# A recurrence's gradient is centred as its last step instead of its first, and an output operand is built by one operation and four copies

## The chip, the cores and the metric

The kernel runs on one core of a Trainium2 chip. Its engines work side by side, each through its own queue in order: TensorE (PE) multiplies matrices, VectorE (DVE), ScalarE (ACT) and GpSimd (POOL) work on elements, SyncE (SP) and some of the others start DMA transfers. The metric is the time of one execution on the device in microseconds, median of several runs. Before the change it is 1993.64 us, the median of 3 runs that lie between 1992.97 and 1996.19 us.

## The reference

Two layers, each `x + attention(norm(x)) + ffn(norm(x))`, all in fp32. The change touches only the first layer's attention, a recurrence ("test-time training") over 32 blocks of 16 tokens, for 4 sequences and 32 heads of width 16:

```python
def step(carry, x):
    W1_s, b1_s = carry
    xq, xk, xv, eta_mb = x
    Z1 = xk @ W1_s + b1_s
    grad = _ln_fused_l2_bwd(Z1, xv - xk, ln_w, ln_b)
    Attn1 = jnp.tril(xq @ xk.swapaxes(-1, -2))
    b1_bar = b1_s - jnp.tril(eta_mb) @ grad
    Z1_bar = xq @ W1_s - eta_mb * Attn1 @ grad + b1_bar
    last_eta = eta_mb[:, :, -1, :, None]
    W1_new = W1_s - (last_eta * xk).swapaxes(-1, -2) @ grad
    b1_new = b1_s - jnp.sum(last_eta * grad, axis=-2, keepdims=True)
    out = xq + _ln(Z1_bar, ln_w, ln_b)
    return ((W1_new, b1_new), out)
```

with the gradient of a layer norm and a squared error:

```python
def _ln_fused_l2_bwd(x, target, gamma, beta):
    mu = x.mean(-1, keepdims=True)
    std = jnp.sqrt(x.var(-1, keepdims=True) + EPS)
    xh = (x - mu) / std
    gxh = (gamma * xh + beta - target) * gamma
    return (D * gxh - gxh.sum(-1, keepdims=True) - xh * (gxh * xh).sum(-1, keepdims=True)) / (D * std)
```

The rest of the first half of the kernel is a gated FFN (hidden size 1408) and the projections around the recurrence. The second layer is an attention with 16 heads over 1024 tokens per pass and a mixture of experts; the change does not touch it.

## The kernel before

**Two stages.** Until about 970 us the kernel computes layer 1; from there, layer 2. Layer 1 goes through the tokens in 8 chunks of 64 tokens of each of the 4 sequences. Every chunk gives 4 steps of the recurrence, 32 steps (n = 0 to 31) in all. The state is small, so a step has few matrix multiplications and a long chain of element operations. The chunk's other work (FFN, projections, post norm of the chunk before) is cut into pieces by generators (`gate_up`, `down`, `keys`, `token_tile`, `queries`, `finish`) and put between the step's parts: `fill(us)` takes pieces from the list until their nominal PE times reach `us`.

```python
for n in range(NM):
    wh = weights_out(n)
    pz = first_product(n, pre)
    po = queries_out(n, wh)
    g = gradient(n, pz, pre)
    gh = out_operands(n, g, pz)
    fill(gaps[0])          # 11 us of other PE work
    update(n, g, pre)
    fill(gaps[1])          # 3 us
    emit_out(n, po, gh)
    fill(gaps[2])          # 8 us
    pre = prepare(n + 1)   # once its chunk's operands are there
```

**One step.** `weights_out` copies the state out of PSUM (tile `wacc`, L332 and L335). `first_product` gives `pz`, the values z beside the attention products, in one PSUM tile (matmuls `pz<-gsum` and `pz<-wq_bd,sk`). `queries_out` starts the output in PSUM tile `pso`. `gradient` (L353 to L391) makes the gradient from z on DVE, with two calls of ACT (a square, L360, and a square root, L364). Each group of 16 values is centred first (L356, L358), then scaled, multiplied by gamma squared and added to the target part (`kv`, L379); then two sums (L382) are taken out (L386 to L388). `update` copies the gradient into the block-diagonal operand `g_bd` (L395, two copies on DVE, two on ACT) and multiplies it into the state (`wacc<-g_bd,km`). `out_operands` makes the two operands of the step's output: `gh` (L421, two POOL operations, one for each half of the head pair, gradient times mask `m2`), and `a_bd` (L424, four DVE operations of 32 partitions each, that add 1 to the attention products in `pz`, multiply them by the negative causal mask `mneg` and put them on a block diagonal). `emit_out` multiplies them (`pso<-a_bd,gh`) and DVE takes the result out (`zch` L449, `bias_o` L450).

**Around it.** `prepare` (L303 to L326) makes the next step's operands on POOL: the DMA `kv<-rows` (L307, on POOL's queue, three buffers), `sk` (L314), the copies of the queries into `wq_bd` (L316, they wait until `queries_out` of the step before has read the old ones) and `km` (L321). At the end of a chunk POOL starts the DMAs `z<-zch` (L454) and `zb<-z` (L456), which bring the recurrence's outputs into another layout. `finish` of that chunk then runs in the next one: ACT squares `zb` (`pn_sq`, L549), PE sums the squares (`pj<-pn_sq,bones`), ACT takes the root (L554), and so on. `gate_up` multiplies into PSUM tile `pf` (two buffers); ACT (`sg`, L477) and DVE (`hid`, L478) empty it.

**What sets the order.** The program above is not the order of the queues. A scheduler reorders each engine's instructions when the kernel is built, by its own estimates of their durations and waits; only those given to `keep_in_program_order` are fixed. So a change in one function can move the instructions of others, on all queues.

## Time and profile before

| what | value |
|---|---|
| median of 3 runs | 1993.64 us |
| the profiled execution's own time | 1996.04 us |
| its span, first to last instruction | 1994.3 us |
| PE busy | 1938.3 us (97%), 11626 matmuls |
| DVE busy | 1169.6 us (59%) |
| ACT busy | 816.1 us (41%) |
| POOL busy | 528.2 us (26%) |
| PE busy, 0 to 100 us | 91.1 us |
| PE busy, 100 to 900 us | 770.1 us |
| PE busy, 900 to 1000 us | 90.6 us |
| PE busy, 1000 us to the end | 986.4 us of 994 |

The span is what the profiler saw of one execution, from the first instruction to the last; the execution's own time lies 1.7 us above it. A busy share is an average; what an engine waits for is read from the waits (engine, line and tile that waited, what released it, total, number, longest) and from the timeline (start, duration, instruction, and in brackets the idle time ahead of it with what ended it). The trace has two matmul records for each fp32 matmul of the program.

### The profile page before, as it was taken

The numbers are of one execution on the slowest core, as the hardware profiler recorded it, in microseconds if no ns is written. First come the engines' busy times: TensorE is split into PE (matmuls) and PEld (weight loads), VectorE is DVE, ScalarE is ACT, GpSimd is POOL, SyncE is SP. The second block draws the span as 40 slices with busy tenths as digits, with TensorE's granted clock in tenths as the row PEclk, the third lists the DMA queues.
The fourth block names the chain that finished last, engine by engine and source line by source line (L and its number), as shares of the span: only waits on it lengthen the run. The fifth ranks groups of instructions, "written<-read, shape, count | busy, mean of one in ns | idle before, by whom it ended". The sixth has DMA issues, their size and how long they took to land.

```text
span 1994.3 us, 32414 instructions
## 1 busy us (share of the span) xinstructions
PE 1938.3 (97%) x11626; PEld 1233.3 (62%) x11626; DVE 1169.6 (59%) x2579; ACT 816.1 (41%) x1695; POOL 528.2 (26%) x643
## 2 busy tenths in 40 slices
PE   8999999999999999998999999999999999999999
PEld 6777676767766676753777744555555555555555
DVE  4445748466666657474555656556555655655565
ACT  2234333334433443422222155455545545555552
POOL 5333343424333342512000101111211121222223
PEclk9999999999999999999999999999999999999999
DMA  6757566646456455745651135444344444333344
GB/s 170 210 130 209 143 185 167 175 120 179 141 145 189 126 173 159 224 128 195 225 168 49 58 94 141 118 106 104 101 111 108 103 110 108 95 101 98 89 115 117
DMA packets 226924, 273.51 MB, mean 137 GB/s; under 512 B 88587, under 2 KB 117452, under 8 KB 226124
## 3 DMA queue, kind: packets, MB, share of 16 engines
q1 hardware_dynamic: 204928, 237.19, 43.3%
q0 software_dynamic: 9760, 28.41, 5.0%
q10 hardware_dynamic: 12076, 5.84, 1.0%
q8 instruction: 93, 1.52, 0.3%
q14 instruction: 67, 0.55, 0.1%
HBM read 174.18 MB, written 34.87 MB: 105 GB/s over the span
## 4 chain that ended last, share of the span: by engine, by line
PE 49%; DVE 1%; DMA 0%; ACT 0%; issue 0%; SPq 0%; DVEq 0%; ACTq 0%
PE pc L1254 11%; PE sc L1207 9%; PE pq L1184 8%; PE px L1301 5%; PE p L1301 4%; PE pk L1184 3%; PE epg L976 3%; PE epo L1039 1%; PE epu L976 1%; PE eox L1069 1%; PE pvo L891 1%; PE pw L866 1%; PE eo L1069 1%; DMA gu<-in_gu 0%; DVE st L1225 0%; ACT prob L1227 0%
## 5 line engine op out<-in xcount | busy, mean ns | idle before, releaser
L1225 DVE TENSOR_REDUCE st<-sc 128x1 f32<-128x512 f32 x256 | 168.9, 681 | 244.0 <-PE sc L1207 244.0
L1227 ACT ACTIVATE prob<-sc,st 128x512 f32<-128x512 f32 x256 | 175.1, 686 | 210.5 <-DVE st L1225 210.3
L1254 PE MATMUL pc<-prT,lv 128*128 128x512 f32 x512 | 230.8, 593 | 0.0
L1232 ACT ACTIVATE prob<-prob,st 128x512 f32<-128x512 f32 x256 | 181.9, 720 | 58.8 <-DVE st L1231 58.8
L1236 DVE STREAM_TRANSPOSE tt<-prob 128x512 f32<-128x512 f32 x256 | 178.4, 700 | 43.0 <-ACT prob L1232 36.5
L117 PE MATMUL pf<-xT,wg 128*128 128x256 f32 x704 | 175.6, 391 | 6.2 <-DMA wg<-in_wg 4.4
L1184 PE MATMUL pq<-cq,uq 128*128 128x512 f32 x384 | 175.2, 592 | 0.0
L117 PE MATMUL pf<-xT,wu 128*128 128x256 f32 x704 | 167.6, 381 | 1.5 <-DMA wu<-in_wu 1.5
L117 PE MATMUL pd<-wd,hid 128*128 128x512 f32 x352 | 166.1, 600 | 1.3 <-DMA wd<-in_wd 1.2
L1254 PEld LDWEIGHTS pc<-prT,lv 128*128 128x128 f32 x512 | 96.4, 190 | 100.1 <-issue 98.1
L117 PEld LDWEIGHTS pf<-xT,wg 128*128 128x128 f32 x704 | 133.2, 194 | 33.5 <-issue 4.7
L1207 PE MATMUL sc<-k,q 32*128 32x512 f32 x1024 | 145.7, 617 | 2.5 <-ACT prob L1227 2.5
L117 PEld LDWEIGHTS pf<-xT,wu 128*128 128x128 f32 x704 | 134.5, 191 | 20.5 <-DMA wu<-in_wu 1.9
L478 DVE SCALAR_TENSOR_TENSOR hid<-pf,us,sg 128x256 f32<-128x256 f32 x88 | 42.0, 478 | 156.9 <-ACT sg L477 156.4
L1184 PEld LDWEIGHTS pq<-cq,uq 128*128 128x128 f32 x384 | 74.1, 193 | 90.7 <-issue 90.0
L314 POOL TENSOR_SCALAR sk<-k,m 128x256 f32<-128x256 f32 x64 | 61.2, 968 | 179.9 <-PE pz L117 167.7
L1195 POOL TENSOR_TENSOR kr<-kr,t2k 128x512 f32<-128x512 f32 x16 | 20.3, 1270 | 332.3 <-DVE t2k L1194 332.3
L421 POOL TENSOR_SCALAR gh<-grad,m 128x256 f32<-128x256 f32 x64 | 61.2, 966 | 154.5 <-DVE grad L390 131.6
L117 PEld LDWEIGHTS pd<-wd,hid 128*128 128x128 f32 x352 | 63.4, 190 | 60.2 <-issue 43.8
L1207 PEld LDWEIGHTS sc<-k,q 32*128 32x128 f32 x1024 | 48.4, 185 | 82.7 <-issue 73.2
L477 ACT ACTIVATE sg<-pf,gs 128x256 f32<-128x256 f32 x88 | 41.6, 473 | 132.8 <-PE pf L117 132.3
L1256 ACT COPY ctxT<-pc 128x512 f32<-128x512 f32 x64 | 37.4, 585 | 127.2 <-PE pc L1254 127.1
(316 smaller groups left out, 3467.9 us busy)
## 6 DMA issues: line engine op xcount, KB each, us to landing
prT<-tt SPq DMA_DIRECT2D x992, 64.0 KB, 2.0
wd<-in_wd SPq DMA_DIRECT2D x176, 256.0 KB, 3.1
wg<-in_wg SPq DMA_DIRECT2D x88, 256.0 KB, 3.0
wu<-in_wu SPq DMA_DIRECT2D x88, 256.0 KB, 3.1
cq<-lat_d SPq DMA_DIRECT2D x48, 256.0 KB, 3.8
rows<-rows SPq DMA_DIRECT2D x128, 66.0 KB, 2.2
kv<-rows POOLq DMA_DIRECT2D x32, 264.0 KB, 4.1
gu<-in_gu SPq DMA_DIRECT2D x3, 2048.0 KB
```

The costliest lines, as they stand in the source:

```text
L117: nc.tensor.matmul(out, lhsT=lhsT, rhs=rhs, start=start, stop=stop, skip_group_check=True)
L314: nc.gpsimd.tensor_scalar_mul(sk[:, :, :, h, :], at(k1[ch], slice(0, P)), m2[:, h : h + 1])
L421: nc.gpsimd.tensor_scalar_mul(gh[:, :, h, :], g, m2[:, h : h + 1])
L976: nc.tensor.matmul(ps, lhsT=w[:, c, :], rhs=x[:, c], start=start and c == 0, stop=c == 1, skip_group_check=True)
L1184: nc.tensor.matmul(ps, lhsT=columns(ws[hg][w]), rhs=x, start=(i == 0), stop=(i == len(srcs) - 1))
L1207: nc.tensor.matmul(ps[h], lhsT=qk[f"q{c}"][r, i * P : (i + 1) * P], rhs=qk[f"k{c}"][r, :], start=(n == 0), stop=(n == 2),)
L1225: pin(nc.vector.tensor_reduce(mx, ps[h], AX.X, ALU.max, negate=True))
L1227: pin(nc.scalar.activation(pr, ps[h], AF.Exp, bias=mx, scale=1.0, accum_out=sm))
L1232: pin(nc.scalar.mul(pr, pr, sm))
L1236: nc.vector.transpose(out=tt[:, :, h - 2], in_=pr.rearrange("p (k kq j) -> p kq k j", kq=4, j=32))
L1254: pin(nc.tensor.matmul(pc, lhsT=lv[:, b, k, :], rhs=at[:, :, k, :], start=(k == 0), stop=(k == E - 1)))
L1301: nc.tensor.matmul(ps[:, q, :], lhsT=a[:, k, q * P : (q + 1) * P], rhs=w[:, k, :], start=start and k == 0 and q == 0, stop=k == 1, skip_gr ...
```

## The change

The gradient is computed in another order. Before, z is centred, squared and scaled, and the mean of the gradient is taken out ahead of the part along z. After, z is squared as it comes out of PSUM; the part along z is taken out first; and the mean of what remains is taken out as the last step. The state W and the bias start centred (`centre(w0)`, `centre(b0)`, L729 to L737, there before the change too), and a gradient that is centred in its last step keeps them so up to rounding, so that z has mean zero without being centred. The two sums, one reduction of 128 x 512 elements before, become two of 128 x 256.

`a_bd` is made by one DVE operation over all 128 partitions into a new tile `at`, and four copies of 32 partitions, two on ACT and two on POOL. `gh` is made by one POOL operation over 512 elements instead of two over 256.

```diff
         def gradient(n, pz, pre):
             z = pz[:, :, :HD]
-            s = wk.tile([P, NG], F32, tag="s", name=f"s_{n}")
-            nc.vector.tensor_reduce(s, z, AX.X, ALU.add)
             xh = wk.tile([P, NG, HD], F32, tag="xh", name=f"xh_{n}", bufs=1)
-            nc.vector.scalar_tensor_tensor(xh, spread(s), -1.0 / HD, z, ALU.mult, ALU.add)
             sq = wk.tile([P, NG, HD], F32, tag="sq", name=f"sq_{n}", bufs=1)
-            nc.scalar.activation(sq, xh, AF.Square)
+            nc.scalar.activation(sq, z, AF.Square)
...
-            nc.vector.tensor_mul(xh, xh, spread(r))
+            nc.vector.tensor_mul(xh, z, spread(r))
...
-            nc.vector.tensor_reduce(
-                s12.rearrange("p k g -> p (k g)"), pair.rearrange("p k g d -> p (k g) d"), AX.X, ALU.add
-            )
+            nc.vector.tensor_reduce(s12[:, 1], pair[:, 1], AX.X, ALU.add)
+            nc.vector.tensor_mul(xh, xh, spread(s12[:, 1]))
             u = wk.tile([P, NG, HD], F32, tag="u", name=f"u_{n}", bufs=1)
-            nc.vector.scalar_tensor_tensor(u, spread(s12[:, 0, :]), -1.0 / HD, pair[:, 0], ALU.mult, ALU.add)
-            nc.vector.tensor_mul(xh, xh, spread(s12[:, 1, :]))
-            nc.vector.scalar_tensor_tensor(u, xh, -1.0 / HD, u, ALU.mult, ALU.add)
+            nc.vector.scalar_tensor_tensor(u, xh, -1.0 / HD, pair[:, 0], ALU.mult, ALU.add)
+            nc.vector.tensor_reduce(s12[:, 0], u, AX.X, ALU.add)
+            nc.vector.scalar_tensor_tensor(u, spread(s12[:, 0]), -1.0 / HD, u, ALU.mult, ALU.add)
...
         def out_operands(n, g, pz):
             gh = wk.tile([P, NG, 2, HD], F32, tag="gh", name=f"gh_{n}")
-            for h in range(2):
-                nc.gpsimd.tensor_scalar_mul(gh[:, :, h, :], g, m2[:, h : h + 1])
-
+            nc.gpsimd.tensor_mul(
+                gh,
+                g.unsqueeze(2).to_broadcast([P, NG, 2, HD]),
+                m2.unsqueeze(1).unsqueeze(3).to_broadcast([P, NG, 2, HD]),
+            )
+            at = wk.tile([P, NG, K], F32, tag="at", name=f"at_{n}", bufs=1)
+            nc.vector.scalar_tensor_tensor(
+                at, pz[:, :, HD:], 1.0, mneg.unsqueeze(1).to_broadcast([P, NG, K]), ALU.add, ALU.mult
+            )
             for be, r in enumerate(quarters):
-                nc.vector.scalar_tensor_tensor(
-                    a_bd[r, :, be, :K],
-                    pz[r, :, HD:],
-                    1.0,
-                    mneg[r].unsqueeze(1).to_broadcast([32, NG, K]),
-                    ALU.add,
-                    ALU.mult,
-                )
+                (nc.scalar.copy if be < 2 else nc.gpsimd.tensor_copy)(a_bd[r, :, be, :K], at[r])
             return gh
```

## The prediction

> **What bounds the kernel now.** I read the page's first part, then TensorE's waits, then the timeline around the long ones.

> ```profile
> PE 1938.3 (97%) x11626; PEld 1233.3 (62%) x11626; DVE 1169.6 (59%) x2579; ACT 816.1 (41%) x1695; POOL 528.2 (26%) x643
> ```

> TensorE is the bound. Only its idle time can be won or added to; the second stage (from 970 us) idles some 10 us in all, and the changed kernel's instruction order, read beside the old one, differs nowhere in it. What TensorE waits for in most of the recurrence (190 to 960 us; total, times, longest):

> ```profile
> PE pj L117 <- ACT pn_sq L549: 5.9, 2, 3.1
> PE pso L117 <- POOL gh L421: 5.8, 4, 2.7
> PE wacc L117 <- DVE g_bd L395: 3.7, 3, 1.7
> PE wacc L117 <- ACT g_bd L395: 1.9, 3, 1.0
> PE pz L117 <- ACT wq_bd L332: 1.8, 2, 1.1
> PE pf L117 <- DVE hid L478: 1.5, 2, 1.1
> ```

> The chain that the change shortens ends in `gh` and `g_bd`: 11.4 us of waits over ten steps. In the other steps filler covers it. Here step 7, TensorE's timeline:

> ```profile
> 264.15 0.48 PE L117 MATMUL pso<-a_bd,gh 128*32 128x68 f32 x17 [2.72 <-POOL gh L421]
> ...
> 267.34 1.93 PE L117 MATMUL pz<-wq_bd,sk 128*32 128x128 f32 x32 [0.79 <-ACT wq_bd L332]
> ...
> 270.05 2.90 PE L117 MATMUL pf<-xT,wg 128*128 128x256 f32 x8
> 274.52 1.89 PE L117 MATMUL pf<-xT,wg 128*128 128x256 f32 x8
> ```

> After the wait of 2.72 the matmuls run slow: 2.90 us for eight against 1.89 later, and `pz` takes 1.93 against 1.08 in other steps. From 265.3 to 272.8 that is 3.0 us lost to the clock on top of the wait. Waits of 2.39 (at 51 us) and 2.23 (at 159) were followed by 2.6 and 1.8 lost; those of 2.2 (at 600) and 3.06 (at 819) by none.

> **The change part by part.** Durations are the groups' means.

> *Gradient.* Gone: sum and centring of z (0.42 each), the double sum (0.68). New: two sums of the shape of L362 (0.42 each), and `at` (0.42), which the new order puts into the chain behind the scaling of `xh`; the four `a_bd` operations were in DVE's pauses. So 1.52 leaves and 1.25 enters: the gradient comes 0.3 us earlier. Where no table load stands between square and root (14 of 32), two `a_bd` operations had also held up the reciprocal (step 31: 0.55 us), so there 0.8. DVE loses 4 x 0.42 + 1.52 - 1.25 = 1.95 us a step, 62 us in all, worth nothing by itself, since TensorE covers it.

> *`gh`.* Two operations of 0.97 become one over 512 elements. POOL's tensor-tensor rows of that size take 1.27 to 1.29 (L495, L496, L1195), two operations with the mask 1.93. I take 1.29, the same operation and count: `gh` comes 0.64 earlier than the gradient gives; at 1.93, not at all.

> *Copies.* Two more on ACT (0.40, row L395) and two on POOL (0.43, row L316). Their readers come later than `gh` in nearly all steps, and the order puts POOL's ahead of `gh`, in its idle time: nothing. They wait for `at`; behind ACT's wait stand table loads and `sg`, which come about 0.2 later, with TensorE a `pf` buffer ahead: nothing. The worst case is 2 us each at the two waits for `hid`.

> *Buffers.* `pz` is held until `at`, 1 us longer, but the next `pz` is 15 us off: nothing.

> *What the chain wins.* Steps 6, 14, 18, 23 lose their waits for `g_bd` (0.5, 1.0, 1.0, 0.5). Step 7: `gh` is 1.0 earlier and the new order has two more matmuls (0.87) ahead of it: 1.85 of 2.72, and the 3.0 of slow clock. `gh` in 13, 17, 21: 0.4, 0.4, 0.9 (fillers ahead of it shrink by 0.3 to 2.3). Step 10: 0.5, since 1.74 of filler leaves. The wait for `hid` in step 12: 0.9, as `hid` now stands ahead of the last gradient operation. Step 30, for a norm: 0.4. Sum: 3.0 + 4.85 + 1.7 + 0.5 + 0.9 + 0.4 = **11.35 won**.

> *What the order loses.* The scheduler moved three things on other queues.

> Step 24: one `pj<-pn_sq` matmul now stands right behind `pso<-wq_bd`, ahead of the gate matmuls.

> ```profile
> 707.29 0.63 PE L117 MATMUL pso<-wq_bd,wh 128*32 128x64 f32 x32
> 716.74 0.65 PE L117 MATMUL wacc<-g_bd,km 128*32 128x64 f32 x32 [1.72 <-DVE g_bd L395]
> 717.82 1.99 PE L117 MATMUL pf<-xT,wg 128*128 128x256 f32 x8 [0.43 <-DVE hid L478]
> ```
> ```profile
> 710.80 1.06 ACT L549 ACTIVATE pn_sq<-zb 128x1024 f32<-128x1024 f32 x1 [0.25 <-DMA zb<-z]
> ```

> `pn_sq` waits for a DMA that the change does not speed up and ends at 711.9; TensorE is there at 707.9: a wait of 4.0, with every later matmul behind it, for 1.72 + 0.43 that go. Net 1.85, and the slow clock.

> Step 28: POOL's `kv` DMA for this very step moves behind two more copies and two `sk` operations.

> ```profile
> 814.27 0.84 POOL L316 COPY wq_bd<-q 32x256 f32<-32x256 f32 x2 [3.87 <-PE pso L117]
> 815.06 0.55 POOL L307 DMA_DIRECT2D kv<-rows  x1
> 816.61 1.82 POOL L314 TENSOR_SCALAR sk<-k,m 128x256 f32<-128x256 f32 x2
> ```
> ```profile
> 818.17 0.18 DVE L367 TENSOR_TENSOR rl<-r,kv 128x16 f32<-128x16 f32 x1 [0.69 <-DMA kv<-rows]
> ```
> ```profile
> 819.53 1.12 PE L117 MATMUL pj<-pn_sq,bones 128*128 128x512 f32 x2 [3.06 <-ACT pn_sq L549]
> 827.49 0.65 PE L117 MATMUL wacc<-g_bd,km 128*32 128x64 f32 x32
> 827.96 0.66 PE L117 MATMUL pso<-a_bd,gh 128*32 128x68 f32 x32
> ```

> Four copies from 814.27 end at 815.95, two `sk` at 817.85; `kv` then lands 3.1 later (815.06 to 818.17 before), at 820.95, and DVE, waiting at L367, holds all behind it. The gradient takes 4.4 more: 825.3. On POOL `km` twice two (2.0, 2.1) and two DMAs (0.6 each) follow `kv`'s landing, then `gh`: 827.5. TensorE reaches the first `pso<-a_bd,gh`, which the new order puts ahead of 16 gate matmuls (6.9 us), at about 818.6, and stands 8.9 us. These, `wacc` and the other outputs then end at 835.5 instead of 828.55; one `pn_sq` matmul (0.87) is done earlier and one of 0.43 later, which leaves **5.7 lost** (with `gh` at 1.93: 6.3).

> Step 25: 0.76 less filler against a gradient that is not earlier, as DVE does the post norm between: 0.6.

> The clock after waits of 4.0 and 8.9: between 0 (the rows of 2.2 and 3.06) and 3.0 each; 3.0 is the row after the longest wait that slowed, and I take it twice. Lost: 1.85 + 5.7 + 0.6 + 6.0 = **14.15**.

> **The sum.** 14.15 - 11.35 = 2.8 us slower: 1998.8 for the profiled execution's 1996.04, which lies 2.4 over the median. On the median: 1996.4. Unseen small losses in an order rewritten on five queues are likelier than unseen gains (all gains lie in the listed waits), so I say **1997.0**.

> [...]

> **Rivals.** *The chain wins.* If the waits at 24 and 28 cost no clock (0 twice) and `kv` in step 28 is no later than before, the losses are 1.85 + 0.6 and about 2 for the moved output matmul: 11.35 - 4.45 = 7 faster, 1986.7. For it: the 3.06 row had no slow clock. Against it: POOL's queue is in order, and `kv` stands behind 2.7 us of named work. It decides at a `kv` landing before 819.

> *`gh` is dear and the clock stays slow.* At 1.93 the gains of 7, 13, 21 shrink by 0.64 each and step 28 loses 0.6 more; with one more slow-clock stretch (3.0) from a new wait, 2.8 + 2.5 + 3.0 = 8.3 slower, 2002. For it: a mask operand, as L421 has; against: the rows of equal operation.

> *The steps all stay covered*, gains and losses both half: 1.4 slower, 1995.

> **How the numbers follow.** 0.2% is 4 us, about what a measurement of this kernel can tell from no change: 1989.65 to 1997.63. The sum with its spread (1993 to 2001) has 0.45, split 0.23 within, 0.22 slower; the chain wins 0.25 (0.02 of it within); the dear `gh` 0.22, slower; all covered 0.08, 0.07 of it within. Faster 0.23, same 0.32, slower 0.45 (0.22 + 0.22 + 0.01). The range leaves out 0.1 on each side: 1987, the chain's win in full, and 2004, the dear case and 2 more.

> **What would show it.** Right: in TensorE's waits a new `pj <- ACT pn_sq` of about 4 us in step 24 and a `pso <- POOL gh` of 8 to 9 in step 28, slow matmuls behind both; `g_bd` waits below 2 us in sum; `gh` at 1.3; the time at DVE down by 62 us with no gain of its own. Wrong: `gh` waits gone altogether, or a chain from `pz` to the gradient that is not shorter (7.8 us in step 12), or new waits for `hid`.

## The result and the profile after

The changed kernel takes 2018.51 us in the median (2015.08 to 2019.25, 4 runs) against 1994.69 for the kernel before (1992.97 to 1996.19, 4 runs): a ratio of 1.0116, 95% interval 1.0099 to 1.0134. It is 23.8 us slower where the prediction's sum had 2.8. Its profiled execution has a span of 2016.6 us, 22.3 more than the one of before. The first part of its page:

```profile
PE 1937.2 (96%) x11626; PEld 1233.8 (61%) x11626; DVE 1132.6 (56%) x2451; ACT 839.2 (42%) x1757; POOL 532.5 (26%) x675
```

TensorE's busy time is the same to 1.1 us (1938.3 before). The whole loss is idle time of TensorE. DVE has 37 us less to do (62 were expected), and that bought nothing, as expected. TensorE's waits from 190 to 960 us (total, times, longest), the view shown for before:

```profile
PE pj L117 <- ACT pn_sq L544: 14.4, 4, 4.5
PE pso L117 <- POOL gh L416: 11.3, 3, 8.9
PE pf L117 <- DMA wg<-in_wg: 4.9, 2, 2.5
PE wacc L117 <- DVE g_bd L391: 3.8, 5, 1.8
PE pf L117 <- DVE hid L473: 2.3, 1, 2.3
```

`pn_sq` went from 5.9 to 14.4, `gh` from 5.8 to 11.3, `hid` from 1.5 to 2.3 (and a wait of 5.5 at 66 us, ahead of this window). `g_bd`, which the change was to shorten, went from 5.6 (3.7 and 1.9) to 3.8. So the chain's waits did shrink, and waits that are not the chain's grew.

Four steps lose 24.3 us between them, what precedes the first step loses 3.9, and the other steps win some of it back. The length of a step here is the time from the end of its `pz` matmuls to the end of the next step's, read off the timelines. The number behind x on TensorE's lines counts records, two for each of these matmuls.

**Step 28** is 12.3 us longer. TensorE, POOL and DVE, from their timelines:

```profile
829.55 1.98 PE L117 MATMUL pj<-pn_sq,bones 128*128 128x512 f32 x4 [2.49 <-ACT pn_sq L544]
840.48 0.43 PE L117 MATMUL pso<-a_bd,gh 128*32 128x68 f32 x2 [8.95 <-POOL gh L416]
840.85 3.78 PE L117 MATMUL pf<-xT,wg 128*128 128x256 f32 x8
844.42 2.13 PE L117 MATMUL pf<-xT,wu 128*128 128x256 f32 x8
```
```profile
826.29 1.93 POOL L314 TENSOR_SCALAR sk<-k,m 128x256 f32<-128x256 f32 x2
828.17 1.15 POOL L307 DMA_DIRECT2D kv<-rows  x2
```
```profile
834.09 0.17 DVE L364 TENSOR_TENSOR rl<-r,kv 128x16 f32<-128x16 f32 x1 [6.66 <-DMA kv<-rows]
```

This is the predicted place: `kv` behind four copies and two `sk`, DVE standing on it for 6.66 us, and one output matmul (of 16) ahead of the gate matmuls, which holds all of them for 8.95 us (8.9 were predicted). The gate matmuls behind it run at half clock (3.78 us for eight records against 1.89; the granted clock is 0.50 until 844.9).

**Step 4** is 5.2 us longer, and the prediction had nothing there. POOL, ACT and TensorE:

```profile
183.13 0.98 POOL L426 COPY a_bd<-at 32x256 f32<-32x256 f32 x2 [8.17 <-DVE at L422]
184.17 1.98 POOL L316 COPY wq_bd<-q 32x256 f32<-32x256 f32 x4
186.25 2.07 POOL L314 TENSOR_SCALAR sk<-k,m 128x256 f32<-128x256 f32 x2
188.26 0.62 POOL L307 DMA_DIRECT2D kv<-rows  x1
188.88 0.78 POOL L451 DMA_DIRECT2D zb<-z  x1
```
```profile
194.74 1.06 ACT L544 ACTIVATE pn_sq<-zb 128x1024 f32<-128x1024 f32 x1 [6.04 <-DMA zb<-z]
```
```profile
195.84 3.31 PE L117 MATMUL pj<-pn_sq,bones 128*128 128x512 f32 x4 [4.54 <-ACT pn_sq L544]
```

POOL stands 8.17 us on `at` with the two new copies at the head of its queue. Behind them wait four copies, two `sk`, `kv` and the transfer of `zb`, which needs none of them. In the kernel before, `zb` was issued at 179.51, 5.9 us after the step's `pz`; here it is 9.1 us after. POOL and TensorE before:

```profile
179.51 0.78 POOL L456 DMA_DIRECT2D zb<-z  x1
```
```profile
185.78 1.98 PE L117 MATMUL pj<-pn_sq,bones 128*128 128x512 f32 x4 [0.93 <-ACT pn_sq L549]
```

**Step 0** is 3.9 us longer: TensorE waits 5.53 us for `hid`, and the next eight records take 3.68. DVE's order puts that `hid` behind the gradient, and the gradient waits 3.67 us for `kv`. TensorE and DVE:

```profile
66.62 3.68 PE L117 MATMUL pf<-xT,wg 128*128 128x256 f32 x8 [5.53 <-DVE hid L473]
```
```profile
59.25 0.18 DVE L364 TENSOR_TENSOR rl<-r,kv 128x16 f32<-128x16 f32 x1 [3.67 <-DMA kv<-rows]
```

**Step 8** is 2.9 us longer by a wait for `hid` too (2.34), there without a wait for `kv`.

A further 3.9 us are lost **ahead of step 0**, where no instruction's place differs. DVE's norm statistics wait for a transfer of the input until 19.75 us (they start at 17.98 before). An operation on `lrb` then takes 4.08 us beside three memsets of POOL (0.15 before, where it ended ahead of them; its line stands in the last section). TensorE waits 1.89 and 0.83 us for `rows`, which stand behind it on DVE, and its granted clock is 0.50 from 29.1 to 32.5 us. That the change makes the transfer late is not shown.

### The profile page after: what moved, and what is told of

Same layout as the page of the kernel before. It is cut to its first block, busy times and chain, and to the rows that moved or that the text cites. A ratio compares the mean times of both kernels' runs of the same rounds, so it can differ in the third digit from the quotient of the medians.

```text
span 2016.6 us, 32397 instructions
## 1 busy us (share of the span) xinstructions
PE 1937.2 (96%) x11626; PEld 1233.8 (61%) x11626; DVE 1132.6 (56%) x2451; ACT 839.2 (42%) x1757; POOL 532.5 (26%) x675
## 3 DMA queue, kind: packets, MB, share of 16 engines
q8 instruction: 93, 1.52, 0.3%
## 4 chain that ended last, share of the span: by engine, by line
PE 48%; DMA 1%; DVE 1%; SPq 1%; ACT 0%; issue 0%; DVEq 0%; ACTq 0%
PE pc L1249 11%; PE sc L1202 9%; PE pq L1179 8%; PE px L1296 5%; PE p L1296 4%; PE pk L1179 3%; PE epg L971 3%; PE epo L1034 1%; PE epu L971 1%; PE eox L1064 1%; PE pvo L886 1%; SPq L1241 1%; DMA prT<-tt 1%; PE pw L861 1%; PE eo L1064 1%; DMA gu<-in_gu 0%
## 5 line engine op out<-in xcount | busy, mean ns | idle before, releaser
L117 PE MATMUL pf<-xT,wg 128*128 128x256 f32 x704 | 176.5, 393 | 15.0 <-DVE hid L473 7.9
L117 PE MATMUL pf<-xT,wu 128*128 128x256 f32 x704 | 166.9, 380 | 0.3 <-DMA wu<-in_wu 0.3
L117 PE MATMUL pd<-wd,hid 128*128 128x512 f32 x352 | 165.5, 599 | 1.7 <-DMA wd<-in_wd 1.6
L117 PEld LDWEIGHTS pf<-xT,wg 128*128 128x128 f32 x704 | 134.0, 195 | 41.6 <-issue 9.6
L117 PEld LDWEIGHTS pf<-xT,wu 128*128 128x128 f32 x704 | 134.2, 191 | 19.2 <-DMA wu<-in_wu 0.7
L314 POOL TENSOR_SCALAR sk<-k,m 128x256 f32<-128x256 f32 x64 | 60.9, 961 | 182.3 <-PE pz L117 172.5
L117 PEld LDWEIGHTS pd<-wd,hid 128*128 128x128 f32 x352 | 63.5, 190 | 59.9 <-issue 44.4
L321 POOL TENSOR_SCALAR km<-kv,m2n 128x256 f32<-128x256 f32 x64 | 60.1, 946 | 101.3 <-PE wacc L117 89.3
```

The source lines that it names most:

```text
L117: nc.tensor.matmul(out, lhsT=lhsT, rhs=rhs, start=start, stop=stop, skip_group_check=True)
L314: nc.gpsimd.tensor_scalar_mul(sk[:, :, :, h, :], at(k1[ch], slice(0, P)), m2[:, h : h + 1])
L321: nc.gpsimd.tensor_scalar_mul(km[:, :, :, h, :], kv[:, :, 0:64].rearrange("p b (al d) -> p b al d", d=HD), m2n[:, h : h + 1])
```

## The experiments

The theory after reading the two traces, called "queue": the arithmetic is about as quick as predicted, and the time goes where the new order puts a transfer, a `hid` or a matmul late on an in-order queue. The rivals: "gradient" (the new gradient costs by itself) and "spread" (the copies and the one-operation mask cost a little in every step). Ratios are to the kernel before on the same chip. This table of step lengths, against the first profile of before, is what the first nine runs are read by; "rest" is all other steps up to the last, "end" what follows the last step's `pz`.

```
              start     0     3     4     8    24  25+26    28   rest    end
changed         3.9   3.9  -1.6   5.2   2.9   2.1   -0.4  12.3   -8.3    2.4
grad_only       1.2   3.2   8.2  -1.1   0.0   4.4    3.0   2.8   -1.7    0.2
ops_only        1.8   5.3  -1.1   1.7   0.4   4.3    0.4   7.9   -7.2   -0.2
held            1.9   3.3  -0.7   0.0   2.7   5.5   -0.5  12.9   -7.7    4.7
kv28            4.0   7.2   0.6   5.9   1.1   5.5   -0.5  -2.4   -5.6    1.5
pin_out         0.6   6.1  -0.2   5.3   1.3   4.7    0.1   2.7   -5.8    1.3
held_pin        1.0   6.2   0.8   0.2   2.7   4.1    1.7   3.0   -8.2   -1.0
before_pin      0.2   0.8  -0.1  -0.2  -1.1   1.1    1.0   3.5   -8.4    1.1
before_2        0.4  -0.1  -0.2  -0.1   0.0  -0.2    0.0   0.0   -0.3    4.3
```

Each row is one profiled execution, and its total need not be that of the median: the execution of `held` took 2018.08 us, 10 over its median, that of `grad_only` 2016.24, 5 under.

### The two halves of the change alone

`grad_only` is before with the new `gradient`; `ops_only` is before with the new `out_operands`.

> Before with the new gradient alone: the mask of the gradient and the four a_bd operations stay as they were. Theory 'queue' (the time is lost where the order of the new instructions puts a transfer or a hid late on an in-order queue, in steps 0, 4, 8 and 28, and three of these come with the a_bd copies): no new wait in steps 0, 4 and 8; in step 28 kv is still issued behind four copies and two sk, but the output matmuls stand behind the 16 gate matmuls again, so at most 3 us there; step 24 keeps its pn_sq wait of about 3.4. Sum near 0: 1990 to 1998. Rival 'gradient' (the new gradient itself costs the time, because the centring at the end or the square of uncentred values lengthens the chain): 2010 or more, with a longer time from pz to the gradient in every step.

> Before with the new out_operands alone (gh by one operation, at by one, four copies); the gradient is the old one. 'Queue': the waits of step 0 (hid, about 5.5 us), step 4 (pn_sq, about 4.5) and step 8 (hid, about 2.3) are there as in the changed kernel, and step 28 has kv behind three copies and the two a_bd copies and ten output matmuls ahead of the gates, so a gh wait of 5 to 9 us: 2008 to 2016. Rival 'gradient': no slower than before, 1990 to 1996. Rival 'spread' (the copies cost in every step, by the longer operations on DVE beside POOL's and by ACT's extra work): also 2008 to 2016, but with the loss spread evenly over the 32 steps and not in four of them.

`grad_only`: 2021.48 (2016.24 to 2025.41), ratio 1.0129 (1.0110 to 1.0149). `ops_only`: 2009.48 (2007.55 to 2014.00), ratio 1.0075 (1.0058 to 1.0092). The first is a miss for "queue" as I had put it: the half that I thought harmless costs as much as the whole. Steps 4, 8 and 28 are as expected, step 0 is not (3.2 us longer), and the largest loss sits in a place that the whole change does not have, step 3. The sign named for "gradient", a longer time from `pz` to the gradient, shows in 19 of the 32 steps (0.2 us in the mean of all) and not in every one. TensorE in step 3:

```profile
154.59 1.02 PE L117 MATMUL pd<-wd,hid 128*128 128x512 f32 x2
163.42 0.32 PE L117 MATMUL pso<-a_bd,gh 128*32 128x68 f32 x1 [7.81 <-POOL gh L417]
...
163.54 0.96 PE L117 MATMUL wacc<-g_bd,km 128*32 128x64 f32 x17
164.42 3.78 PE L117 MATMUL pf<-xT,wg 128*128 128x256 f32 x8
```

One output matmul and nine of `wacc` stand ahead of the gate matmuls, and the first of them waits for `gh`, as in step 28 of the whole change: 7.81 us of waiting and slow matmuls behind it (3.78 us for eight records against 1.89), in a step that is 8.2 us longer. And in step 28, where `grad_only` has `kv` as late as the whole change but the output matmuls behind the gates, the loss is 2.8, not 12.3. So in step 28 most of the price comes with the place of that one matmul, given a late `kv`; an early `kv` with the matmul ahead of the gates was not run. `ops_only` shows the losses of steps 4 and 28 in smaller sizes and that of step 0 in a larger one; step 8 lost 0.4 (a wait for `hid` of 1.42, where about 2.3 was expected), and step 24's 4.3 (a wait of 3.56 for `g_bd`) was not expected.

### Moving single things back

`held` queues POOL's two copies behind `kv` and `zb`; of the 5920 instructions on TensorE's queue 4 change places.

```
+    for d in dmas.values():                # the last kv and the last zb
+        behind.enter_context(tc.issue_after(d.ins))
     for be, r in enumerate(quarters):
         (nc.scalar.copy if be < 2 else nc.gpsimd.tensor_copy)(a_bd[r, :, be, :K], at[r])
```

> The changed kernel, with POOL's two a_bd copies queued behind the kv transfer of their own step and behind the last zb transfer; no instruction added or taken away. 'Queue': the pn_sq wait of step 4 goes back to about 0.9 and the hid wait of step 0 shrinks by about 1 us or goes; step 28 stays as it is: 2007 to 2013. 'Spread': the copies cost the same wherever they stand: 2016 to 2020.

2008.06 (2004.46 to 2018.08), ratio 1.0073 (1.0048 to 1.0099). Step 4's loss is gone. POOL and TensorE:

```profile
182.50 0.61 POOL L307 DMA_DIRECT2D kv<-rows  x1
183.11 0.78 POOL L455 DMA_DIRECT2D zb<-z  x1
185.82 1.13 POOL L417 TENSOR_TENSOR gh<-grad,m 128x512 f32<-128x512 f32 x1 [1.93 <-DVE grad L386]
187.01 0.84 POOL L430 COPY a_bd<-at 32x256 f32<-32x256 f32 x2
```
```profile
190.19 1.98 PE L117 MATMUL pj<-pn_sq,bones 128*128 128x512 f32 x4 [0.92 <-ACT pn_sq L548]
```

The copies are the same two, and in this step cost nothing behind `gh`. The profiled execution lost as much again elsewhere (against the changed kernel 3.4 us in step 24, where TensorE's order is the same, and 2.3 behind the last step), so what the median won is not read off this trace's total. The wait of step 0 goes from 5.53 to 4.26 only: the copies made 1.3 of it.

`kv28` queues two `wq_bd` copies of step 28 behind its `kv`; 24 of TensorE's 5920 instructions change places, all in that neighbourhood, and the output matmuls come behind the gates again.

```
+    with tc.issue_after(dmas["kv"].ins) if n == 28 and al >= 2 else ExitStack():
         nc.gpsimd.tensor_copy(wq_bd[r, :, al, HD:]..., at(q1[ch], r))
```

> The changed kernel, with the last two wq_bd copies of step 28 alone queued behind that step's kv transfer on POOL, which puts kv (and zb) ahead of them, and with it the order puts the output matmuls of step 28 behind the gates again; no instruction added or taken away. 'Queue': the gh wait of 8.9 us in step 28 goes, with the slow matmuls behind it, and nothing before 800 us changes: 12 us less, 2004 to 2009. 'Spread': 2015 to 2020.

2010.74 (2004.64 to 2015.34), ratio 1.0075 (1.0052 to 1.0098), 2 us above the range. Step 28 loses nothing (-2.4 against +12.3). "Nothing before 800 us changes" did not hold in its profile: waits for the weights' transfers of 3.29 at 87 us and 3.30 at 517 us took part of it back, at places where no order differs.

`pin_out` leaves `kv` late and queues the output matmuls of each step behind that step's last `wacc` matmul.

```
+    with tc.issue_after(last[0].ins):       # the last wacc matmul of this step
         for al in range(4): ...             # the output matmuls
```

> The changed kernel, with the output matmuls of every step (pso from a_bd and gh) queued on TensorE behind that step's last wacc matmul; nothing else is pinned, and kv in step 28 stays behind four copies and two sk. If one output matmul ahead of the gate matmuls makes the loss of step 28 (12.3 us against before): the wait of 8.9 for gh goes, the 16 gate matmuls run under it, and at most 3 us of the step's loss are left, as in the kernel with the gradient alone, whose output matmuls stand there: 2007 to 2011. If the late kv makes it wherever the matmul stands: the wait comes back at the gates (for hid) or at wacc (for g_bd), 2015 to 2020.

2013.58 (2008.01 to 2019.06), ratio 1.0087 (1.0059 to 1.0116). The total falls between the two ranges, but step 28 goes to +2.7. TensorE there:

```profile
838.34 1.89 PE L117 MATMUL pf<-xT,wu 128*128 128x256 f32 x8
...
841.79 1.89 PE L117 MATMUL pf<-xT,wu 128*128 128x256 f32 x8
843.99 0.65 PE L117 MATMUL wacc<-g_bd,km 128*32 128x64 f32 x32 [0.30 <-DVE g_bd L391]
```

DVE still stands 6.11 us on `kv`, and TensorE waits 0.30. With `kv` as late, that gives 9.6 of the 12.3 us to the place of the output matmuls. "Spread" had 2015 to 2020 for `held` and `kv28` and falls with their 2008 and 2011.

### Holding the orders together, and the kernel before again

`held_pin` is the whole change with `held` and `pin_out`, and the `pn_sq` matmuls at their place in the program. `before_pin` is the kernel before with the last two. `before_2` is the kernel before, profiled once more.

> The changed kernel with three orders held: the output matmuls behind wacc, the pn_sq matmuls at their place in the program on TensorE, and POOL's two a_bd copies behind kv and zb. The arithmetic is that of the changed kernel. If the order is what costs: the losses of step 28 (9.5 of 12.3), of step 4 (5.2) and of step 24 (2) go, those of steps 0 and 8 (about 6) stay, so 1997 to 2004. If the new arithmetic costs by itself: 2008 or more.

> The kernel before with the same two orders held on TensorE (it has no copies on POOL to hold). By the theory that the order decides, little goes: the waits for gh ahead of wacc in steps 7, 13 and 21 become waits for g_bd, and the pn_sq wait of step 28 (3.06) goes: 1988 to 1996. Its distance to the changed kernel with orders held is what the new arithmetic is worth under like orders: within 8 us of each other if the order is what costs, 15 or more apart if the arithmetic is.

> The kernel before, unchanged, profiled once more: how far one profile of it lies from another. If the 3.8 us that the changed kernel loses ahead of step 0, where no instruction differs, are chance, then this profile lies up to 4 us from the first one there; if the changed program causes them, this one is within 0.5 us of the first.

`held_pin`: 2003.04 (1997.95 to 2006.33), ratio 1.0032 (1.0018 to 1.0045): three orders give back two thirds of the loss with the arithmetic untouched. Not all of that undoes the change's own loss, since two of these orders alone make the kernel before 5 us faster. `before_pin`: 1992.06 (1989.61 to 2002.46), ratio 0.9974 (0.9957 to 0.9992), the one version here that beats both kernels, and it has none of the change in it. The 11 us between the two fall between the bounds that I had set and decided nothing; steps 0, 8 and 24 make 12 of them. `before_2` lies 0.4 us from the first profile at the start and within 0.2 in the steps named in the table, but 4.3 behind the last step, and steps 16 and 20 differ by 1.5 and -1.6. Nor is one repeat a bound on chance: step 24 is 2.1 longer in the changed kernel and 5.5 in `held`, with the same order of TensorE there. The start is 0.2 and 0.4 in two more profiles of the old arithmetic and 0.6 to 4.0 in those with new parts, though their code there is the same.

### The same matmul order for all four combinations

In these four, every matmul of the recurrence and its fillers is held in the order of the program, so that TensorE's order is the same matmul by matmul (0 of 5920 differ).

```
     ins = nc.tensor.matmul(out, ...)
+    if held[0]:                             # set before the first filler
+        tc.keep_in_program_order(ins)
```

> The kernel before, with every matmul of the recurrence and of its fillers held on TensorE in the order in which the program writes them; the orders on the other queues are left to the scheduler. This is the base of a square of four kernels whose TensorE order is the same, matmul by matmul, so that what is left between them is the arithmetic and the other queues. No output matmul or pn_sq matmul stands ahead of its planned place, so not slower than before by more than its unplanned waits: 1985 to 2000.

> The same TensorE order, with the new gradient alone. If the 20 us that the new gradient cost alone came from the matmul put ahead in step 3 and the rest of TensorE's order: within 5 us of the kernel before with this order. If the new gradient costs by itself (its work behind kv is 0.36 us longer, the a_bd operations stand in its chain): 8 us or more slower than that.

> The same TensorE order, with the new out_operands alone. POOL's two a_bd copies still stand ahead of the zb transfer of step 4: a pn_sq wait there of 3 us or more and 2 to 6 us of loss, and little else: 0 to 7 us slower than the kernel before with this order. If the copies cost in every step: 10 or more.

> The same TensorE order, with the whole change. If TensorE's order made most of the 23.8 us: the loss of step 4 (about 5) stays, the rest of it goes, and the shorter chain gives 0 to 4 back: 0 to 8 us slower than the kernel before with this order. If the arithmetic or the copies cost by themselves: 15 or more slower.

```
before_prog  2067.49  1.0353 (1.0335 to 1.0371)
grad_prog    2065.98  1.0341 (1.0322 to 1.0360)
ops_prog     2071.51  1.0371 (1.0343 to 1.0399)
after_prog   2078.06  1.0398 (1.0374 to 1.0421)
```

The base is a miss: the program's order is 72 us slower than the scheduler's, with waits of 7 to 8 us for `g_bd` in steps 17 and 21. As a square it works. The gradient that cost 26 us alone in the scheduler's order costs nothing here (-1.5, intervals overlapping): "gradient" falls for this order. What the arithmetic costs in the scheduler's order, 72 us faster and with other waits, it does not show. `ops_prog` is 4.0 us slower, as expected. The whole change costs 10.6 us instead of 23.8, a little over the bound for "queue". In its trace two `pn_sq` waits are longer, 7.63 us in step 4 and 5.44 in step 8 (4.70 and 0.69 in `before_prog`), where `zb` is behind the copies again. These steps are 2.8 and 7.5 us longer, but step 9 is 6.9 shorter, and the two profiled executions (2068.91 us, the fastest of five, and 2070.16, the slowest of four) do not differ by the 10.6 us of the medians. So the traces do not place these.

`held_prog` adds `held` to `after_prog`:

> The whole change in TensorE's order as the program writes it, with POOL's two a_bd copies also queued behind kv and zb. What is left between the whole change and the kernel before in this order is 10.6 us in the medians, with longer pn_sq waits in steps 4 and 8 (7.6 and 5.4 against 4.7 and under 2). If the copies ahead of zb make it: those waits go back, and 5 to 10 of the 10.6 us go, a ratio of 1.035 to 1.038 to the kernel before (1.0353 for the old arithmetic in this order, 1.0398 for the new). If the copies' own time or the slower operations of DVE beside POOL make it: 1.039 or more.

2061.21 (2055.28 to 2067.14), ratio 1.0323 (1.0306 to 1.0341). More than all of the 10.6 us goes; the two waits are 4.78 and 0.91. With TensorE's order fixed and the copies behind the transfers, the new arithmetic is not slower than the old (1.0323 against 1.0353, the intervals overlapping a little). That it is faster is not shown.

### The mask by one operation, by itself

`gh_pin` is `before_pin` with the one-operation mask and nothing else of the change. The order of TensorE, DVE and ACT is the same to the instruction.

> The kernel before with TensorE's two orders held, and of the change only the mask of the gradient by one operation of POOL; every queue has the order of the kernel before with these orders held. gh is then some 0.8 us shorter (1.07 against 1.9), which is worth at most that in the few steps that wait for gh (step 28: 4.1), and DVE's g_bd copies and gsum get longer beside it (about 0.2 each): a ratio of 0.995 to 0.998 to the kernel before, against 0.9974 without it. If the operation itself costs, by the operations of DVE beside it: 1.000 or more.

1997.96 (1994.64 to 2002.64), ratio 1.0004 (0.9992 to 1.0016), against 0.9974 (0.9957 to 0.9992) without it: no gain, and perhaps some 6 us of cost. The groups of DVE and POOL, `before_pin` and then `gh_pin` (busy time, mean ns of one):

```profile
L395 DVE COPY g_bd<-grad 32x256 f32<-32x256 f32 x64 | 24.9, 390 | 1.2
```
```profile
L395 DVE COPY g_bd<-grad 32x256 f32<-32x256 f32 x64 | 40.0, 625 | 1.2
```
```profile
L420 POOL TENSOR_TENSOR gh<-grad,m 128x512 f32<-128x512 f32 x32 | 34.8, 1087 | 150.1 <-DVE grad L390 139.5 <-DVE ln_mv L135 5.3 <-DVE rows L289 5.2
```

`gh` is 0.86 us shorter (1.09 against two of 0.975). The two `g_bd` copies that DVE runs at the same moment take 0.47 longer together, and `g_bd` feeds `wacc`, which in most steps TensorE reaches before `gh`'s matmuls. In `gh_pin` the waits for `g_bd` in steps 10, 18 and 23 grew by 0.5 to 0.8 each; the profiled pair, 3.2 us apart, differs besides by 1.6 ahead of step 0 and by waits for weights in steps 3 and 8 (0.8 and 1.5), which are not shown to come from the mask.

## Why the prediction was wrong, point by point

**The listed terms came out near in sum, by errors that cancel.** Won, by step lengths: `g_bd` in 6, 14, 18, 23 2.2 (3.0 predicted); `gh` in 13, 17, 21 2.3 (1.7; step 17 lost 0.7); step 12 1.4 (0.9); step 30 1.5 (0.4); step 10 0.1 (0.5); step 7 1.2 (4.85, of which the slow clock, 0.50 from 265.1 to 271.9 before, lies partly in step 8). That is 8.7 against 11.35. Lost: step 24 2.1 (1.85 and 3.0 of clock), step 25 -0.8 (0.6), step 28 12.3 (5.7 and 3.0). That is 13.6 against 14.15. By these alone the kernel would be 5 us slower, and the prediction said 2.8, while steps 7 and 28 were each off by about 3.6 us. Of the 22.3 us by which the profiled executions' spans differ, 5 are these, 12 are steps 0, 4 and 8, which the sum does not have, 3.9 are the start and 2.4 follow the last step, where two profiles of the kernel before differ by 4.3. The steps not named win 0.9.

**The step that failed is a term costed at nothing.** "Their readers come later than `gh` in nearly all steps, and the order puts POOL's ahead of `gh`, in its idle time: nothing." The engine was idle; its queue was not empty. I asked who reads the copies, and not what stands behind them while they wait for `at`: the transfers of `zb` and `kv`. In step 4 POOL stood 8.17 us on `at` with these behind it, and TensorE's wait for `pn_sq` went from 0.93 to 4.54: 5.2 us, gone in `held`, whose ratio is 1.0073 instead of 1.0116. The comparison with TensorE's order fixed shows it a second time (`held_prog` against `after_prog`, 1.0323 against 1.0398). The same prediction did use this reasoning in step 28.

**"The worst case is 2 us each at the two waits for `hid`"** failed too. The waits are 5.5 and 2.3, each followed by half clock (the granted clock is 0.50 from 63.2 to 70.1 and from 288.5 to 291.9 us; the next eight records take 3.68 and 3.64). In step 8 both orders moved: `sg` stands behind ACT's copies, which wait for `at`, and DVE's `hid` behind the gradient and `gsum`. In step 0, the wait for `by_ch` (2.39 before) became 0.85, so TensorE came earlier to a `hid` that was not earlier: that one came 1.4 us later after `pz`. What was won at the first wait was lost at the second. The copies made about 1.3 us of that second wait (4.26 in `held`); in `grad_only`, without copies, it is still 4.43.

**Step 28** was right in place and mechanism, and 3.6 us too small. Two terms were off: `kv` landed 5.9 us after its issue (828.17 to 834.09) and not 3.1, and two `pn_sq` matmuls stand ahead of the wait, not one. The 3.1 was one row, near the shortest: the median of the changed kernel's 32 `kv` transfers is 4.6. Why the one of step 28 takes longer (5.6 and 6.0 in `grad_only` and `held` too) stays open; two issued together are not enough, since a pair in step 0 of the kernel before landed after 3.1 and 3.2. That the wait came out at 8.95 where 8.9 was reckoned is luck: TensorE reached it 2.8 us later after `pz` than reckoned, and `gh` was 2.8 later too. The clock behind it cost 2.1, not 3.0.

**Step 24**: the `pn_sq` wait is 3.43 (4.0 predicted), with no slow clock in this profile (the granted clock is 1.0 from 291.9 to 834.7 us, and the next eight gate records take 1.89); the other kernels with the new gradient had 4.0 to 4.7 there.

**Step 7**: "`gh` is 1.0 earlier" failed. It came 10.79 us after `pz` against 10.65 before. The order moved a `yf` addition of POOL beside the chain, and `rl` (0.11 to 0.38 in other steps) took 1.19 next to it:

```profile
266.43 0.69 DVE L489 TENSOR_TENSOR yf<-pd,dsc 128x512 f32<-128x512 f32 x1 [1.44 <-PE pd L117]
...
267.31 1.19 DVE L364 TENSOR_TENSOR rl<-r,kv 128x16 f32<-128x16 f32 x1
```
```profile
267.20 1.26 POOL L491 TENSOR_TENSOR yf<-yf,xr 128x512 f32<-128x512 f32 x1 [1.22 <-DVE yf L489]
```

**`gh` at 1.29** was too dear (1.08), and the price that the step did not have is DVE's: `g_bd` from 0.39 to 0.57, `gsum` from 0.54 to 0.64. The gain of 62 us on DVE came out as 37: of the 25 that are missing, 14.6 are these two, 3.9 `lrb` at the start and 2.3 `rl`.

**The chain from `pz`** is shorter as predicted (step 12: 7.55 against 7.79; in 26 of 32 steps). Where `kv` is what comes last, it is longer: from `rl`'s start to the end of the gradient 4.16 in step 0 of `grad_only` against 3.79 before and 3.80 in `ops_only`, since a second sum now stands behind `kv`'s addition. I had measured the chain from one end only.

**The rivals.** "The chain wins" decided at a `kv` landing before 819 in step 28. It landed at 834; this kernel was already some 10 us late there, so that is about 824 by the clock of the kernel before, and the rival fell. "Dear `gh`" was right that a new wait brings a slow stretch (0.50 from 834.7 to 844.9 us), and wrong in the reason. "All covered" fell with the waits of steps 0, 4 and 8. Of the signs named for a wrong prediction one came, new waits for `hid`; of those for a right one, `g_bd` waits below 2 us did not (3.8).

## What to carry to other kernels

When an instruction is added to an in-order queue, cost it by what stands behind it while it waits, transfers first, and not by the engine's idle time or by its own reader. When a scheduler orders the queues, look through the new order for matmuls put ahead of the fillers that were to cover their inputs: one output matmul so placed went with 8 to 12 us in each of two places here, about as much as all that the arithmetic was to win. To judge the arithmetic, hold the order the same in both kernels; alone, each half of a change is a new draw of the order.

## What the runs showed of the hardware

**DVE's `g_bd` copies took longer beside POOL's two-operand mask than beside its mask by a scalar.** With `tensor_scalar` on POOL (`before_pin`) they took 0.39 us in the mean, with `tensor_tensor` (`gh_pin`) 0.63, at an unchanged order. In step 7 of the changed kernel the second copy ends 0.15 us after `gh`. What makes the copies longer is not shown. Ahead of step 0 of the changed kernel a DVE operation on 128x16 elements took 4.08 us beside three memsets of POOL and ended with the last of them (24.66 and 24.63 us). The first memset began 0.40 us after that operation's start. In `gh_pin`, where it began 0.33 us after, the operation took 4.02; in the kernel before, where it began 1.01 us after, it took 0.15.

```profile
20.58 4.08 DVE L708 TENSOR_SCALAR lrb<-lrb 128x16 f32<-128x16 f32 x1
```
```profile
20.98 1.82 POOL L743 MEMSET wq_bd<- 128x2048 f32 x1
...
23.61 1.02 POOL L743 MEMSET a_bd<- 128x1088 f32 x1
```
